# Layer 3's attention: causal masks of the weights by GpSimd selects, and the division's transposes one step later

## The chip, the cores and the metric

The kernel runs on one core of a Trainium2 chip. Its engines are named here as in the profile: PE is TensorE (PEld its weight loads), DVE is VectorE, ACT is ScalarE, POOL is GpSimd, SP is SyncE. Each works through its own queue in order, and they wait for each other through semaphores. The metric is the device time of one execution in microseconds (us), as the median of several runs.

## The reference

The reference is a chain of four layers on x of shape 16 x 256 x 128 (sequences of 256 tokens). Each layer normalises x and adds an attention-like part and a feed-forward part, both computed from the same normalised x. The change concerns the attention of layer 3, which is causal with 16 heads of 8 columns:

```python
q, k, v = (proj(Wq), proj(Wk), proj(Wv))
scores = jnp.einsum('bhsd,bhtd->bhst', q, k)
mask = jnp.triu(jnp.ones((S, S), dtype=bool), k=1)
scores = jnp.where(mask, -jnp.inf, scores)
attn = jax.nn.softmax(scores / sqrt(D), axis=-1)
out = jnp.einsum('bhst,bhtd->bhsd', attn, v)
```

Layer 1 has the same kind of attention, and the kernel uses the same function `attention` for both. The third layer's feed-forward part follows its attention in the program.

## The kernel before

The 16 sequences lie in 8 blocks of two. `attention` goes over 16 half-blocks `(i, bl)`, one sequence each, in a software pipeline: in pass `s` of its loop, `now` is the half-block whose maxima are taken, `last` (the one before) gets its weights, and `old` (two before) gets its context. The 16 half-blocks need 18 passes. The queues of PE, ACT and DVE keep the order in which the code is written (`manual_schedule`).

The keys of a sequence are cut into 4 chunks of 64. The parts are worked in three steps, each with some of the chunks, so that only the lower triangle and the blocks on its diagonal are computed:

- `maxima` (L857) forms the scores with queries on the partitions (tile `sc`), and DVE takes the largest of each row from them (`M`, L878). Step 0 handles chunk 3, step 1 chunks 2 and 0, step 2 chunk 1. After step 2 the maxima are copied, negated, to `negm` (L882).
- `shift` (L887) transposes `negm` by PE (`mT`, L893), and DVE adds it to the queries (`Q2`, L899 and L902). From here on the row's maximum is taken off by the matmul itself.
- `weights` (L904) forms the scores again, now with keys on the partitions (tile `se`), and ACT takes the exponential of them (`E`, L920) from PSUM to SBUF, in two halves `n` of 2 groups of heads. Step 0 handles chunk 0, step 1 chunks 3 and 1, step 2 chunk 2. `E` has one buffer for each step.
- `context` (L922) multiplies the `vals` by `E` of all three steps (tile `av`), in the order step 0, step 1 twice, step 2; a column of ones in `vals` gives the sum of the weights. ACT copies the result to `cu` (L935).
- `divide` (L937) transposes `cu` by four PE transposes (L942), and DVE takes the reciprocal of the sums (L947) and multiplies (L948) into `cx`. `turn` (L953) transposes a block's `cx` once both halves are there (`cxT`, L957).
- `project` (L799) makes the queries, keys and values of the next block, in five portions (`pq` twice, `pk` twice, `pv`), which are put between the steps. A pass with an even `s` has both portions `pq` and the turn, one with an odd `s` both portions `pk` and `pv`. ACT copies them to `Qp` (L810), `Qm` (L812), `Kp` (L817) and `vals` (L833), and DVE makes `Km` from `Kp` (L819). The last two half-blocks have no projections beside them.

Both `maxima` and `weights` call `score` (L836). All PE matmuls go through `mm` (L111). After its matmuls, `score` adds the causal mask to the diagonal blocks by four more matmuls: `pick`, a selector, times `after` or `before`, a 64 x 64 triangle of -1e30, both in bf16. They accumulate into the same PSUM tile and close its accumulation:

```python
for g in (0, 2, 1, 3):
    r = slice(64 * (g // 2), 64 * (g // 2) + 64)
    o = cut(tiles[g // 2][:, g % 2, :])
    ...
    mm(o, pick[r], m.to_broadcast([64, *o.shape[1:]]), False, True)
```

PSUM is divided into two single banks, which `av`, `cu`, `pq`, `pk`, `pv` and `cxT` take in turn, and three pairs of banks, which `sc` (two pairs a step), `se` (two pairs a step) and `mT` (one) take in turn. A tile can be written only when the tile three turns earlier has been read.

In the loop, step 0 of a pass issues the maxima of `now`, the context of `old`, the weights of `last`, the division of `old`, and a portion of the projection; step 1 the maxima, a portion and the weights; step 2 the maxima, a portion or a turn, and the weights; then comes the shift. In layer 3 `beside` adds small reductions on DVE (`gx`, L1133) between the steps of the first passes.

Of the kernel before, what the change touches and what calls it, by code (L numbers as in the profile page):

```python
# [13 lines left out]
ALU = mybir.AluOpType  # L14
# [5 lines left out]
B, S, D = 16, 256, 128  # L20
NBLK = 8
NT = 4
E = 8
# [28 lines left out]
def program(ctx: ExitStack, tc: tile.TileContext, x, consts, consts0, rows, pk0, w0s, w0e, pk1, pk1i, pk2, pk3, out):  # L52
    nc = tc.nc
# [6 lines left out]
    def bank(name):  # L60
        return psum["now"].tile([P, 512], F32, tag="ps", name=name)

    def pair(name):
        return psum["pairs"].tile([P, 2, 512], F32, tag="pr", name=name)
# [45 lines left out]
    def mm(o, l, r, start=True, stop=True):  # L110
        nc.tensor.matmul(o, l, r, start=start, stop=stop)  # L111
# [43 lines left out]
    for n in range(2):  # L155
        t = cp.tile([P, 4, 2, 4, 2, 16], F32, tag=f"negm{n}", name=f"negm{n}")
# [5 lines left out]
    for n in range(2):  # L162
        t = cp.tile([P, 8, 8, 2, 16], F32, tag=f"vals{n}", name=f"vals{n}")
# [5 lines left out]
    pick, after, before = (cp.tile([P, n], BF16, tag=k, name=k) for k, n in (("pick", 128), ("after", 64), ("before", 64)))  # L169
# [19 lines left out]
    with early, banks(8, 0), tc.tile_pool(name="l0", bufs=2) as sp:  # L189
# [15 lines left out]
        for hf in range(2):  # L205
# [3 lines left out]
            n = TILES * SLOTS // P  # L209
# [196 lines left out]
        parts = {}  # L406
# [283 lines left out]
        with tc.manual_schedule(engines=ordered):  # L690
# [10 lines left out]
            for n in range(4):  # L701
                nc.sync.dma_start(
                    out=yT[:, :, 4 * n : 4 * n + 4, :],
                    in_=ycd.rearrange("d (h b t) -> d h b t", h=2, b=B)[:, :, 4 * n : 4 * n + 4, :],
                )
        with tc.manual_schedule(engines=ordered | {mybir.EngineType.Pool}):
# [7 lines left out]
            for k in range(NJ):  # L714
                if k + AHEAD < NJ:
                    fetch_weights(k + AHEAD)
                n = k - TILES - 1
# [66 lines left out]
    def attention(ap_, kp_, blocks, w, layer, beside=iter(())):  # L784
# [51 lines left out]
        def score(tiles, lhs, rhs, parts, wide, cut, mask):  # L836

            for T in range(2):
                for c, at, k0, k1 in parts:
                    for g in range(4):  # L840
                        r = slice(32 * g, 32 * g + 32)
                        o = T * wide + at
                        mm(
                            tiles[g // 2][:, g % 2, o : o + k1 - k0],
                            lhs[r, T, c].rearrange("p j k -> p (j k)"), rhs[r, T, k0:k1], T == 0 and at == 0, False,
                        )
            for g in (0, 2, 1, 3):
                r = slice(64 * (g // 2), 64 * (g // 2) + 64)
                o = cut(tiles[g // 2][:, g % 2, :])
                m = mask[r]  # L850
                for _ in o.shape[1:-1]:
                    m = m.unsqueeze(1)
                mm(o, pick[r], m.to_broadcast([64, *o.shape[1:]]), False, True)
# [33 lines left out]
        def shift(i, bl):  # L887

            t, name, o = blk[i], f"{layer}_{i}_{bl}", bl * S
            ps = pair(f"mT_{name}")  # L890
            for T in range(2):
                for c in range(4):
                    nc.tensor.transpose(  # L893
                        ps[:, T, c * P : (c + 1) * P], negm[bl][:, c, T].rearrange("p g j k -> p (g j k)"), ident
                    )
            Q2 = t["Q2", bl] = ap_.tile([P, 2, S], F32, tag="Q2", name=f"Q2_{name}")
            q2 = Q2.rearrange("p t (c q) -> p t c q", c=4)
            mT = ps.rearrange("p t (c j q) -> p t c j q", c=4, j=2)
            nc.vector.tensor_tensor(  # L899
                q2, t["Qp"][:, :, o : o + S].rearrange("p t (c q) -> p t c q", c=4), mT[:, :, :, 0, :], ALU.add  # L900
            )
            nc.vector.tensor_tensor(q2, q2, mT[:, :, :, 1, :], ALU.add)  # L902

        def weights(i, bl, step):  # L904

            t, name = blk[i], f"{layer}_{i}_{bl}"
            parts, cut = (
                (((0, 0),), lambda a: halves(a)[:, :, 0:64]),
                (((3, 0), (1, 64)), lambda a: halves(a)[:, :, 0:128].rearrange("p t (n c) -> p t n c", n=2)),
                (((2, 0),), lambda a: halves(a[:, 0:256])[:, :, 0:64]),  # L910
            )[step]
            se = [pair(f"se{step}{n}_{name}") for n in range(2)]
            wide = 128 if step == 2 else 256
            E = t["E", bl, step] = ap_.tile([P, 4, 2 * wide], F32, tag=f"E{step}", name=f"E{step}_{name}", bufs=1)
            score(
                se, t["Km"][:, :, 4 * bl : 4 * bl + 4], t["Q2", bl],
                [(c, at, 64 * c, S) for c, at in parts], wide, cut, before,
            )
            for n in range(2):
                nc.scalar.activation(E[:, 2 * n : 2 * n + 2, :], se[n][:, :, 0 : 2 * wide], AF.Exp, scale=ISQ)  # L920

        def context(i, bl):  # L922
            t, name = blk[i], f"{layer}_{i}_{bl}"
            ps = bank(f"av_{name}")
            for n, (c, step, at, wide) in enumerate(((0, 0, 0, 256), (1, 1, 64, 256), (3, 1, 0, 256), (2, 2, 0, 128))):
                nq = 256 - 64 * c
                for T in range(2):
                    for g in range(4):
                        mm(
                            ps[32 * g : 32 * g + 32, (T + 1) * S - nq : (T + 1) * S],  # L930
                            vals[i % 2][:, 4 * bl + c, 4 * T + g].rearrange("p j k -> p (j k)"),
                            t["E", bl, step][:, g, T * wide + at : T * wide + at + nq], n == 0 and T == 0, n == 3 and T == 1,
                        )
            cu = t["cu", bl] = ap_.tile([P, 2, S], F32, tag="cu", name=f"cu_{name}")
            nc.scalar.copy(cu, ps.rearrange("p (t q) -> p t q", t=2))  # L935

        def divide(i, bl):  # L937
            t, name = blk[i], f"{layer}_{i}_{bl}"
            ps = bank(f"cu_{name}")
            for c in range(2):  # L940
                for T in range(2):
                    nc.tensor.transpose(  # L942
                        ps[:, (2 * c + T) * P : (2 * c + T + 1) * P], t["cu", bl][:, T, c * P : (c + 1) * P], ident
                    )
            p3 = ps.rearrange("p (h k) -> p h k", k=16)
            rd = ap_.tile([P, 32, 1], F32, tag="rd", name=f"rd_{name}")
            nc.vector.reciprocal(rd, p3[:, :, 8:9])  # L947
            nc.vector.tensor_tensor(  # L948
                t["cx"][:, 2 * bl : 2 * bl + 2, :].rearrange("p c (h k) -> p (c h) k", k=8), p3[:, :, 0:8],
                rd.to_broadcast([P, 32, 8]), ALU.mult,  # L950
            )

        def turn(i):  # L953
            name = f"{layer}_{i}"
            ps = transpose4(blk[i]["cx"], f"cxT_{name}")
            cT[i] = kp_.tile([P, 512], F32, tag="cT", name=f"cT_{name}", bufs=NBLK)
            nc.scalar.copy(cT[i], ps)  # L957

        seqs = [(i, bl) for i in blocks for bl in range(2)]
        with tc.manual_schedule(engines={mybir.EngineType.PE, mybir.EngineType.Activation, mybir.EngineType.DVE}):  # L960
            for _ in project(blocks[0]):
                pass
            coming = iter(())
            turns = []
            for s in range(len(seqs) + 2):
                now, last, old = (seqs[k] if 0 <= k < len(seqs) else None for k in (s, s - 1, s - 2))
                if now and now[1] == 0 and now[0] != blocks[-1]:
                    coming = project(blocks[blocks.index(now[0]) + 1])
                for step in range(3):
                    if now:  # L970
                        maxima(*now, step)
                    if step == 0 and old:
                        context(*old)
                    if step == 2 and s % 2 == 0:
                        if turns:
                            turn(turns.pop())
                    elif step > 0:
                        next(coming, None)
                    if last:
                        weights(*last, step)  # L980
                    if step == 0:
                        if old:
                            divide(*old)
                            if old[1] == 1:
                                turns.append(old[0])
                        next(coming, None)
                    if step < 2:
                        next(beside, None)
                if now:
                    shift(*now)  # L990
                next(beside, None)
            for i in turns:
                turn(i)
# [119 lines left out]
    with tc.tile_pool(name="l3w", bufs=1) as wp:  # L1113
# [31 lines left out]
        with banks(4, 0), tc.tile_pool(name="l3t", bufs=4, space=PSUM, reuse_waits="tile") as tp, \  # L1145
                tc.tile_pool(name="l3", bufs=2, reuse_waits="tile") as sp:
            base = wp.tile([P, B], F32, tag="base", name="base")
# [345 lines left out]
```

## Time and profile before

| what | value |
|---|---|
| median of 3 runs | 1593.74 us (1591.17 to 1594.62) |
| the profiled execution's own time | 1487.93 us |
| its span, first to last instruction | 1486.2 us |
| granted TensorE clock over the span | 0.94 of full speed |
| layer 3's attention in the span | about 1085 to 1386 us |
| one pass with `pq` at full clock (1300.77 to 1316.97) | 16.2 us |
| one pass with `pk` at full clock (1182.46 to 1199.56) | 17.1 us |

The profile is that of one execution. It gives the busy time of each engine, the waits of one engine for another, the chain of work that ended last, and a timeline of all instructions. In a timeline row stand the start in us from the span's start, the duration in us (with idle time inside a merged row left out or not much), the engine, the line, the operation, the tiles written and read with their shapes, the count, and in brackets the idle time of the engine just before it and what ended that. PEld rows are the better guide to PE's order, since the ends of matmuls are modelled. The profiled execution is shorter than the runs that give the median.

### The profile page before, as it was taken

What the parts mean: (1) busy time and instruction counts of PE and PEld (TensorE: products, weight loads), DVE (VectorE), ACT (ScalarE), POOL (GpSimd) and SP (SyncE); (2) the same over time, 40 slices, a digit from 0 to 9 for tenths busy, and PEclk for the clock granted to TensorE, in tenths of its full rate; (3) what the DMA queues carried; (4) which work ended last, traced back from release to release, by engine and by line L of the source; (5) the groups of instructions that cost most, each with busy time, mean ns of one, the idle gap of its engine ahead of it and who ended that gap; (6) DMA issues with size and microseconds to landing.
All of it is one profiled execution on the core that took longest, in us unless ns stands there. A gap on an engine that the chain in (4) does not pass through costs nothing.

```text
span 1486.2 us, 28149 instructions
## 1 busy us (share of the span) xinstructions
PE 1340.1 (90%) x11950; PEld 868.6 (58%) x11950; DVE 752.8 (51%) x1636; ACT 578.4 (39%) x898; POOL 214.3 (14%) x218
## 2 busy tenths in 40 slices
PE   3659999969898999899999999999979999999995
PEld 3546899836565666656555445554546666666434
DVE  7355444756666555335732336423375565554364
ACT  5412223334353554321343334333344545543551
POOL 1366004323110000000220112211100000000013
PEclk9979999977798999899999999999978999997998
DMA  7849669640000000000000000000000000000001
GB/s 225 283 135 312 205 178 278 197 152 21 10 11 2 2 2 2 2 1 1 0 1 0 1 0 1 0 0 0 0 1 2 2 2 2 2 2 2 1 1 57
DMA packets 71007, 77.92 MB, mean 52 GB/s; under 512 B 7649, under 2 KB 60258, under 8 KB 70242
## 3 DMA queue, kind: packets, MB, share of 16 engines
q1 hardware_dynamic: 66210, 66.39, 14.5%
q0 software_dynamic: 4240, 8.99, 1.8%
q8 instruction: 94, 1.54, 0.4%
q10 hardware_dynamic: 432, 0.75, 0.2%
q14 instruction: 31, 0.25, 0.1%
HBM read 55.46 MB, written 20.64 MB: 51 GB/s over the span
## 4 chain that ended last, share of the span: by engine, by line
PE 79%; DVE 10%; ACT 7%; issue 2%; DMA 1%; POOL 1%; POOLq 0%; DVEq 0%; SPq 0%; ACTq 0%
PE h L111 15%; PE se L111 9%; PE sc L111 8%; PE po L111 7%; PE av L111 5%; ACT E L920 4%; DVE M L878 3%; PE c L111 3%; PE mT L893 3%; PE sy L111 3%; PE sg L111 2%; PE su L111 2%; PE pq L111 2%; PE pv L111 2%; PE b L111 2%; PE a L111 2%
## 5 line engine op out<-in xcount | busy, mean ns | idle before, releaser
L878 DVE TENSOR_REDUCE M<-sc 128x4 f32<-128x1024 f32 (+3 forms) x256 | 195.9, 818 | 105.0 <-PE sc L111 105.0
L111 PE MATMUL h<-h,pk 128*128 128x512 f32 x512 | 221.0, 592 | 0.0
L920 ACT ACTIVATE E<-se 128x1024 f32<-128x1024 f32 (+1 forms) x192 | 158.8, 879 | 126.0 <-PE se L111 125.7
L111 PEld LDWEIGHTS h<-h,pk 128*128 128x128 f32 x512 | 97.3, 190 | 119.0 <-issue 114.8
L111 PE MATMUL sc<-Kp,Qm 32*128 32x192 f32 (+3 forms) x2048 | 139.8, 358 | 25.0 <-ACT E L920 19.9
L111 PE MATMUL se<-Q,Km 32*128 32x256 f32 (+3 forms) x2048 | 138.4, 355 | 22.4 <-DVE M L878 20.9
L111 PEld LDWEIGHTS sc<-Kp,Qm 32*128 32x128 f32 x2048 | 103.5, 207 | 74.6 <-ACT E L920 33.4
L111 PEld LDWEIGHTS se<-Q,Km 32*128 32x128 f32 x2048 | 99.3, 202 | 62.9 <-issue 51.8
L1098 ACT ACTIVATE h<-h,pk 128x512 f32<-128x512 f32 x64 | 44.0, 687 | 144.3 <-PE h L111 144.2
L1048 POOL TENSOR_TENSOR pr<-q,k 128x512 f32<-128x512 f32 (+2 forms) x24 | 28.3, 1205 | 495.7 <-ACT k L1041 285.8
L601 POOL DMA_INDIRECT yk<-YS,slots x64 | 60.7, 949 | 225.9 <-DMA YS<-ys 95.0
L1108 DVE TENSOR_TENSOR x<-x,po 128x512 f32<-128x512 f32 x8 | 5.5, 688 | 170.5 <-PE po L111 170.5
L111 PE MATMUL av<-E,vals 128*32 128x256 f32 (+3 forms) x2048 | 77.7, 304 | 0.0
L389 POOL DMA_INDIRECT XS<-xn,slots x64 | 63.0, 985 | 73.4 <-DVE slots L368 48.3
L1240 POOL TENSOR_TENSOR xT<-xT,c 128x512 f32<-128x512 f32 x8 | 10.2, 1271 | 389.8 <-DVE c L1239 380.4
L935 ACT COPY cu<-av 128x512 f32<-128x512 f32 x32 | 18.8, 586 | 120.6 <-PE av L111 120.6
L111 PEld LDWEIGHTS av<-E,vals 128*32 128x32 f32 x2048 | 52.9, 111 | 20.0 <-issue 1.6
L583 DVE TENSOR_TENSOR hs<-hs,su 128x512 f32<-128x512 f32 x46 | 31.6, 686 | 57.3 <-PE su L111 57.3
L899 DVE TENSOR_TENSOR Q<-Qp,mT 128x512 f32<-128x512 f32 x32 | 22.0, 688 | 58.0 <-PE mT L893 58.0
L111 PE MATMUL pk<-xT,pk 128*128 128x512 f32 x80 | 47.0, 672 | 3.8 <-ACT Qm L812 3.7
L819 DVE TENSOR_SCALAR Km<-Kp,consts 128x512 f32<-128x512 f32 x64 | 32.2, 545 | 34.6 <-ACT Kp L817 34.6
L111 PEld LDWEIGHTS sy<-we,hs 128*128 128x128 f32 x368 | 47.6, 192 | 2.4 <-DVE hs L583 0.5
(276 smaller groups left out, 2259.0 us busy)
## 6 DMA issues: line engine op xcount, KB each, us to landing
we<-in_w0e SPq DMA_DIRECT2D x46, 384.0 KB, 3.9
toe<-kd SPq DMA_DIRECT2D x32, 512.0 KB, 6.8
xs<-XS SPq DMA_DIRECT2D x46, 128.0 KB, 4.4
YS<-ys SPq DMA_DIRECT2D x46, 128.0 KB, 2.6
XS<-Z SPq DMA_DIRECT2D x4, 1024.0 KB, 9.8
pk<-in_pk SPq DMA_DIRECT2D x1, 3145.5 KB
x<-in_x SPq DMA_DIRECT2D x8, 256.0 KB, 5.2
ycd<-yc SPq DMA_DIRECT2D x8, 256.0 KB, 8.4
```

The lines of the kernel that those rows point to most:

```text
L111: nc.tensor.matmul(o, l, r, start=start, stop=stop)
L389: d = nc.gpsimd.indirect_dma_start(out=XS[hf][:, :], out_offset=at_rows(slots[:, hf, k, n : n + 1]), in_=xn[HALVES[hf][n // NT]][:, n % NT ...
L583: nc.vector.tensor_tensor(h, h, pu, ALU.mult)
L601: nc.gpsimd.indirect_dma_start(out=y, out_offset=None, in_=YS[hf][:, :], in_offset=at_rows(slots[:, hf, k, n : n + 1]),)
L819: nc.vector.tensor_scalar(t["Km"][:, T, :, j, :], chunks(t["Kp"][:, T, :]), C["hmask"][:, j : j + 1], C["hone"][:, j : j + 1], ALU.mult, A ...
L878: nc.vector.tensor_reduce(dst, src, AX.X, ALU.max, negate=True)
L893: nc.tensor.transpose(ps[:, T, c * P : (c + 1) * P], negm[bl][:, c, T].rearrange("p g j k -> p (g j k)"), ident)
L899: nc.vector.tensor_tensor(q2, t["Qp"][:, :, o : o + S].rearrange("p t (c q) -> p t c q", c=4), mT[:, :, :, 0, :], ALU.add)
L920: nc.scalar.activation(E[:, 2 * n : 2 * n + 2, :], se[n][:, :, 0 : 2 * wide], AF.Exp, scale=ISQ)
L935: nc.scalar.copy(cu, ps.rearrange("p (t q) -> p t q", t=2))
L1048: nc.gpsimd.tensor_tensor(pr[:, :, j:], q[:, :, j:], k[:, :, 0 : S - j], ALU.mult)
L1098: nc.scalar.activation(hn[:, c, :], ps, AF.Gelu, scale=W2[sn][:, c : c + 1])
```

## The change

In layer 3 alone (`late`), `score` is called without a mask for the weights, and the last ordinary matmul closes the accumulation. The exponential is thus taken of unmasked scores. After each of its two halves, POOL sets the entries above the diagonal to zero in place, with `affine_select` on each diagonal block: one instruction for each half of the partitions (`j`), over 2 groups, 2 tiles of heads and 64 queries. That makes 4 of them in step 0, 8 in step 1 and 4 in step 2. The maxima keep their masks, and so does all of layer 1.

Also in layer 3, `divide` is called at the end of step 1, after the weights of step 1, instead of in step 0 after the weights of step 0. So its transposes stand on PE between `se` of step 1 and `sc` of step 2, and its two DVE instructions between the maxima of step 1 (and `Km`) and those of step 2. The single banks are taken in the new order.

```diff
@@ score @@
-                            lhs[r, T, c].rearrange("p j k -> p (j k)"), rhs[r, T, k0:k1], T == 0 and at == 0, False,
+                            lhs[r, T, c].rearrange("p j k -> p (j k)"), rhs[r, T, k0:k1], T == 0 and at == 0,
+                            mask is None and T == 1 and at == parts[-1][1],
                         )
+            if mask is None:
+                return
             for g in (0, 2, 1, 3):
@@ attention @@
+        late = layer == 3
@@ weights @@
-                [(c, at, 64 * c, S) for c, at in parts], wide, cut, before,
+                [(c, at, 64 * c, S) for c, at in parts], wide, cut, None if late else before,
             )
             for n in range(2):
                 nc.scalar.activation(E[:, 2 * n : 2 * n + 2, :], se[n][:, :, 0 : 2 * wide], AF.Exp, scale=ISQ)
+                if late:
+                    for _, at in parts:
+                        d = E.rearrange("p g (t q) -> p g t q", t=2)[:, 2 * n : 2 * n + 2, :, at : at + 64]
+                        for j in range(2):
+                            r = slice(64 * j, 64 * j + 64)
+                            nc.gpsimd.affine_select(
+                                out=d[r], in_=d[r], pattern=[[0, 2], [0, 2], [1, 64]], compare_op=ALU.is_ge, fill=0.0,
+                                base=0, channel_multiplier=-1,
+                            )
@@ the loop @@
                     if last:
                         weights(*last, step)
+                    if old and step == (1 if late else 0):
+                        divide(*old)
+                        if old[1] == 1:
+                            turns.append(old[0])
                     if step == 0:
-                        if old:
-                            divide(*old)
-                            if old[1] == 1:
-                                turns.append(old[0])
                         next(coming, None)
```

## The prediction

> **What bounds the kernel now.** I read the page first (engine shares, clock), then the waits and the timeline of layer 3's attention (1085 to 1386 us of the span).
>
> ```profile
> PE 1340.1 (90%) x11950; PEld 868.6 (58%) x11950; DVE 752.8 (51%) x1636; ACT 578.4 (39%) x898; POOL 214.3 (14%) x218
> PE 79%; DVE 10%; ACT 7%; issue 2%; DMA 1%; POOL 1%; POOLq 0%; DVEq 0%; SPq 0%; ACTq 0%
> ```
>
> PE is the engine to shorten; POOL runs nothing between the last product of layer 2 and 1408.7 us, so the whole attention of layer 3 has an idle GpSimd. A busy PE is not yet a bound, so I ask what PE waits for in this stage (columns: us in total, times, longest):
>
> ```profile
> PE sc L111 <- ACT E L920: 9.7, 13, 0.8
> PE se L111 <- DVE M L878: 4.2, 9, 1.1
> PE mT L893 <- DVE negm L882: 3.2, 5, 2.5
> ```
>
> Three short waits recur: the third maxima (sc of step 2) wait for the exponentials of step 1, because the three pairs of banks go round; the second weights wait for the maxima; the transposes mT wait for negm. One period at full clock, from av at 1300.77 to the next av at 1316.97, shows where they lie:
>
> ```profile
> 1303.22 0.59 ACT L935 COPY cu<-av 128x512 f32<-128x512 f32 x1 [3.78 <-PE av L111]
> 1304.16 0.11 PEld L111 LDWEIGHTS <-pick 64*128 64x128 bf16 x4 [0.33 <-issue]
> 1304.38 0.42 PEld L942 LDWEIGHTS cu<-consts,cu 128*128 128x128 f32 x4
> 1304.54 1.94 ACT L920 ACTIVATE E<-se 128x1024 f32<-128x1024 f32 x2 [0.73 <-PE se L111]
> 1304.77 0.30 PEld L111 LDWEIGHTS pq<-xT,pk 128*128 128x128 f32 x2
> ...
> 1310.24 0.11 PEld L111 LDWEIGHTS <-pick 64*128 64x128 bf16 x4 [0.22 <-issue]
> 1310.57 0.30 PEld L111 LDWEIGHTS sc<-Kp,Qm 32*128 32x128 f32 x4 [0.21 <-issue]
> 1310.73 1.94 ACT L920 ACTIVATE E<-se 128x1024 f32<-128x1024 f32 x2 [0.41 <-PE se L111]
> 1311.81 0.52 PEld L111 LDWEIGHTS sc<-Kp,Qm 32*128 32x128 f32 x12 [0.94 <-ACT E L920]
> ...
> 1314.10 0.39 DVE L882 COPY negm<-M 64x32 f32<-64x32 f32 x2
> 1314.16 0.11 PEld L111 LDWEIGHTS <-pick 64*128 64x128 bf16 x4
> 1314.61 0.86 PEld L893 LDWEIGHTS mT<-consts,negm 128*128 128x128 f32 x8 [0.33 <-PE se L111]
> ```
>
> The four masks of a step hold PE for 0.22 us (1304.16 to 1304.38) or 0.33 us (1310.24 to 1310.57), and delay the exponential behind them; the division's transposes hold PE for 0.39 us (1304.38 to 1304.77) where PE has other work ready; and a hole of about 0.8 us lies just before 1311.81, where it has none.
>
> **What the Trainium skill says.** "Perfetto Trace Analysis", section "GPSIMD Engine Instruction", asks that POOL be timed by start-to-start spacing and not by the reported span. I do so below; here both agree within 0.1 us. "GPSIMD Engine Reference", section 2.1, says that a core of GpSimd goes on to the next instruction once its own 16 partitions are done, so the selects on partitions 0 to 63 and 64 to 127 might overlap. The trace does not support it: the four 64-partition memsets of L166 start 0.24 to 0.28 us apart and last 0.20 to 0.24. I count no overlap. Section 8 there says that GpSimd contends with VectorE instructions that have two SBUF inputs or a two-port mode. The trace agrees: L1069 takes 1.73 us beside POOL and 0.68 without. In this stage DVE's maxima and divisions read PSUM, and Km (L819) reads one tensor at about one element per cycle (541 ns for 512), so I take no slowdown.
>
> **The change part by part.** In layer 3 it removes 12 masks per half-block (4 in each of 3 steps, 16 half-blocks, 192 in all), adds 4, 8 and 4 selects per half-block (256 in all) on POOL, and moves four transposes, one reciprocal and one product from step 0 to the end of step 1. No DMA moves and SP's queue is untouched. In the built order context's first matmuls of each E wait for POOL, and so does the next exponential into the same E, which context precedes anyway.
>
> *Period with pq (the one shown).* Step 0: 0.22 of masks and 0.39 of transposes leave, so pq and sc of step 1 come 0.61 earlier. The maxima follow, and se of step 1 ends at 1310.24 - 0.61 = 1309.63. The exponential then starts about 0.13 us later (as the copy of av starts 0.13 after the next load, 1303.09 to 1303.22) instead of 0.49 later: 1309.76; ACT is free of Qm at 1310.32 - 0.61 = 1309.71. Its first half lets sc go on 1.08 later, at 1310.84 instead of 1311.81: 0.97 gained. The transposes (0.39) fit into the hole and cost nothing; were the hole gone they would cost their 0.39. Step 2: its mask of 0.22 gives nothing, because the maxima of step 2 and negm (until 1314.49) end last; they move with sc. Gain 0.95.
>
> *Period with pk* (av at 1182.46 to 1199.56). PE again gains 0.6 in step 0, but the chain exponential E0 (1186.23) - Kp - Km - first maxima (until 1190.89) - se sets the time, and only the mask ahead of E0 shortens it: 0.25. PE's wait for M grows instead. At step 1 the mask's 0.36 is added. Gain 0.6. DVE has room for the division there: it idles 1.87 us before the maxima of step 2 at 1194.85, and reciprocal and product take 0.36 + 0.42.
>
> *Sum of PE's side.* 7 periods with pk x 0.6, 6 with pq x 0.95, and the two without projections x 0.6 (they wait for E and M as the pk periods do): 4.2 + 5.7 + 1.2 = 11.1 us.
>
> *The selects.* The trace has no select; its nearest rows, in the timeline of POOL:
>
> ```profile
> 1463.79 0.41 POOL L1268 TENSOR_TENSOR m<-xn,b 128x128 f32<-128x128 f32 x1 [12.03 <-DVE b L1218]
> 1464.16 0.77 POOL L1268 TENSOR_TENSOR m<-xn,nb 128x128 f32<-128x128 f32 x2
> 1465.37 1.05 POOL L1269 TENSOR_TENSOR xn<-xn,a 128x512 f32<-128x512 f32 x1
> 1466.38 0.41 POOL L1268 TENSOR_TENSOR m<-xn,b 128x128 f32<-128x128 f32 x1
> ```
>
> Each select covers 64 partitions x 256 elements. From below: memsets of 1024 start 0.89 apart, 0.87 ns an element, with 0.16 fixed: 0.38 us. From the middle: products L1268 of 128 start 0.37 apart and L1269 of 512 1.01, so 0.16 + 1.67 ns an element: 0.58 for 256 with two inputs. "GPSIMD Engine Reference", section 7, gives 1.03 to 2.03 cycles per element for compare-and-select code, an estimate of 0.38 to 0.59 with 1.2 GHz and 0.16 fixed. From above: the nb form of L1268 takes 0.85 for only 128. I take d = 0.5, with 0.38 and 0.85 as ends.
>
> *What hides them.* In the pq period the first half of E1 is ready at about 1310.8; then 8 selects of E1 and 4 of E2 follow on POOL. Context starts at 1316.97 - 0.95 = 1316.0 and comes to E2 after about 1.8 us of its 2.3: 1317.8. So 12d must fit in 7.0: d up to 0.58. In the pk period 1193.2 to 1200.7 gives 0.62. At d = 0.5 the cover holds. If it is gone, each period loses 12 x (d - 0.6), and everything behind context on PE (se of step 0, then ACT and DVE) is late by it. The gain is used up at about d = 0.6 + 0.75 / 12 = 0.66.
>
> *The end.* The last half-block has no maxima beside it: the first half of E1 is ready at about 1379.3, context wants E2 at about 1382, and 12d = 6.0 ends at 1385.3. Against the end of av before (1383.2) this puts the end about 2.6 later (1.4 at 0.4, 3.7 at 0.59).
>
> Sum: -11.1 + 2.6 = -8.5 us on a profiled execution of 1487.93 us (span 1486.2). The median of the runs, 1593.74, is 1.071 times that; no view shows why, but where the clock is low in this trace (0.74 to 0.90 in some periods) masks take 0.40 instead of 0.28, so the saving should stretch about as much: -9. **Forecast 1585.**
>
> **The rivals.** *POOL is late* (slower). One mechanism: d above 0.66, so that context waits for the last selects of E2 in each period. At d = 0.75: 12 x 0.15 = 1.8 less 0.75 is +1.05 a period, x 15 = 16, plus about 5.5 at the end: +21, 1615. At 0.85: +34 and 6.5, 1634. For it: POOL's slow 0.85 us product, and that runs of 64 in a four-dimensional pattern may cost more than a memset's. Against it: a select has one input, and the two-input row gives 0.58. *Nothing left* (within noise): d near 0.63 to 0.66, or Km doubled by POOL's port traffic in the seven pk periods; in full, at the 2.5 times of L1069, it would cost 7 x 1.5 = 10 and undo the gain: about 1593. *The change doesn't do what it says*: excluded by the built order, in which the 192 masks are gone and the transposes stand after se of step 1 (in layer 1 nothing moves).
>
> **How the numbers follow.** The noise of a measurement of this kernel is about 0.2%, 3 us. Gain with cover: 0.58, its own range 1579 to 1590 (d from 0.4 to 0.6, low clock in more periods). Nothing left: 0.09. POOL late: 0.33, of which about half lies below 1616. Range 1576 to 1616: leaves out some 0.17 above and 0.02 below. The likeliest is the gain, 1585.
>
> **What would show it.** Right: selects starting under 0.6 us apart; no wait of av for POOL beyond the last half-block; the wait of sc for E down from 9.7 to a few us while that of se for M grows; periods of about 15.3 (pq) and 16.5 us (pk) at full clock instead of 16.2 and 17.1; negm still the last before mT. Wrong: a wait "av <- POOL E" of a microsecond or more in every period (POOL late), Km well over 541 ns (contention), or sc of step 2 waiting as long as before although the transposes stand there.

## The result

The changed kernel takes 1581.54 us (median of 11 runs, 1579.75 to 1586.72) against 1593.28 us before on the same chip (11 runs). The ratio is 0.9939 with a 95% interval of 0.9914 to 0.9964, which is 9.7 us less, between 5.7 and 13.7. Here and below a saving in us is this ratio applied to the median before; the medians themselves differ by some us more or less than that (here by 11.7 us). The forecast was 1585, 8.7 us less than its base of 1593.74.

The profiled execution of the changed kernel took 1582.27 us (span 1580.6). It is not to be set beside the 1486.2 us of the span before: the products `s` of layer 2 start at 830.1 us here and at 723.8 us before, so the difference had arisen ahead of layer 2, where the change touches nothing. From there to the last of them it is 321.5 us in both. It goes with the chip: the kernel before takes 1593.23 us (median) on the chip of e1 to e4, but 1487.86 and 1489.71 us on those of e5 to e8 and of e9 and e10. What follows compares layer 3's attention alone, pass by pass.

The page of the changed kernel, engine shares and the row of the selects:

```profile
PE 1353.3 (86%) x11758; PEld 872.0 (55%) x11758; DVE 755.0 (48%) x1636; ACT 577.1 (37%) x898; POOL 318.9 (20%) x474
L932 POOL TENSOR_SCALAR_AFFINE_SELECT E<-E 64x256 f32<-64x256 f32 x256 | 105.8, 413 | 211.4 <-ACT E L925 200.1
```

There are 192 matmuls less on PE and 256 more instructions on POOL, at 413 ns each. The idle time of POOL ahead of them is nearly all waiting for ACT. What PE waits for in the attention of layer 3 (total, times, longest), first before (1085 to 1386 us), then in the changed kernel (1178 to 1478 us):

```profile
PE sc L111 <- ACT E L920: 10.8, 15, 0.8
PE se L111 <- DVE M L878: 5.3, 10, 1.1
PE mT L893 <- DVE negm L882: 3.2, 5, 2.5
```

```profile
PE se L111 <- DVE M L881: 8.6, 10, 1.1
PE mT L896 <- DVE negm L885: 7.6, 14, 2.5
PE sc L111 <- ACT E L925: 2.4, 3, 0.9
PE av L111 <- POOL E L932: 2.0, 3, 1.3
```

(The prediction shows 9.7 and 4.2 us for the first two before: its rows are those of a window from 1085 to 1345 us, and not to 1386.) The wait of `sc` for the exponentials has gone from 10.8 to 2.4 us. The waits for the maxima and for `negm` have grown in its place, and `av` waits for POOL only three times, all in the last half-block. One pass with `pq`, and the one with `pk` behind it, in the timeline:

```profile
1277.47 1.94 ACT L925 ACTIVATE E<-se 128x1024 f32<-128x1024 f32 x2
1277.48 0.42 PEld L957 LDWEIGHTS cu<-consts,cu 128*128 128x128 f32 x4 [0.23 <-issue]
1278.06 0.30 PEld L111 LDWEIGHTS sc<-Kp,Qm 32*128 32x128 f32 x4 [0.17 <-issue]
1278.54 0.52 PEld L111 LDWEIGHTS sc<-Kp,Qm 32*128 32x128 f32 x12 [0.18 <-ACT E L925]
1278.56 5.54 POOL L932 TENSOR_SCALAR_AFFINE_SELECT E<-E 64x256 f32<-64x256 f32 x12 [3.65 <-ACT E L925]
...
1280.84 0.52 DVE L885 COPY negm<-M 64x32 f32<-64x32 f32 x2
1281.47 0.86 PEld L896 LDWEIGHTS mT<-consts,negm 128*128 128x128 f32 x8 [0.69 <-PE se L111]
...
1283.78 2.11 PEld L111 LDWEIGHTS av<-E,vals 128*32 128x32 f32 x64
...
1289.81 1.19 DVE L819 TENSOR_SCALAR Km<-Kp,consts 128x512 f32<-128x512 f32 x2 [3.53 <-ACT Kp L817]
1290.92 2.47 DVE L881 TENSOR_REDUCE M<-sc 128x4 f32<-128x768 f32 x4
...
1292.31 1.10 PEld L111 LDWEIGHTS se<-Q,Km 32*128 32x128 f32 x28 [0.96 <-issue]
```

The transposes `cu` now lie where the hole was: the load of `sc` waits 0.18 us for E instead of 0.94. The twelve selects from the first half of E1 on take 5.54 us, 0.46 each, and end at 1284.1, 1.5 us before context comes to E2. In the pass with `pk` the loads of `se` stand idle for 0.96 us (PE's matmuls for 0.85) until the maxima behind Km are done, as foreseen.

The passes from one start of `av` to the next were read from the timelines of all profiles. The 16 starts bound 15 passes. The first twelve have projections beside them, six with `pq` and six with `pk`; the table has these twelve. "Full clock" is the length to which most agree within 0.03 us; the last column is what the twelve have above it in all.

| kernel | pq, full clock | pk, full clock | passes over 0.2 us longer | surplus |
|---|---|---|---|---|
| before | 16.19 | 17.10 | 4 | 6.1 us |
| e5_before_again | 16.19 | 17.10 | 5 | 7.6 us |
| changed | 15.35 | 16.59 | 1 | 1.5 us |
| e1_masks_only | 15.55 | 16.59 | 4 | 6.5 us |
| e2_move_only | 15.97 | 17.10 | 0 | 0.0 us |
| e4_no_selects | 15.19 | 16.36 | 0 | 0.0 us |
| e6_step2_and_last_on_PE | 15.35 | 16.59 | 0 | 0.0 us |
| e7_Km_later, e8_both | 15.36 | 15.79 | 0 | 0.0 us |
| e9_filler | 16.19 | 17.10 | 0 | 0.0 us |

So the twelve passes lost 12.6 us between the two profiles: 6 x 0.84 and 6 x 0.51, which is 8.1 us, at full clock, and 4.6 us of surplus. The second part was not in the forecast. The last three passes took 2.3 us less, at a clock of 0.74 to 0.99 in both profiles, and the end behind them took 3.2 us more. In all, from the first start of `av` to the first loads of the next stage, 255.2 us became 243.5. The experiments are about these parts. (Where the expectations of e5 and e6 count 15 passes up to a "sixteenth start of av", their figures are those of 14 passes and of the fifteenth start.)

### The profile page after: what moved, and what is told of

Same layout as the page of the kernel before. It is cut to its first block, busy times and chain, and to the rows that moved or that the text cites. A ratio compares the mean times of both kernels' runs of the same rounds, so it can differ in the third digit from the quotient of the medians.

```text
span 1580.6 us, 28021 instructions
## 1 busy us (share of the span) xinstructions
PE 1353.3 (86%) x11758; PEld 872.0 (55%) x11758; DVE 755.0 (48%) x1636; ACT 577.1 (37%) x898; POOL 318.9 (20%) x474
## 4 chain that ended last, share of the span: by engine, by line
PE 74%; DVE 10%; ACT 6%; issue 5%; another core or an unknown queue 4%; POOL 1%; DMA 1%; POOLq 0%; DVEq 0%; SPq 0%; ACTq 0%
PE h L111 14%; PE sc L111 7%; PE se L111 7%; PE po L111 7%; PE av L111 5%; DVE M L881 4%; PE c L111 3%; ACT E L925 3%; PE mT L896 3%; PE sg L111 3%; PE sy L111 2%; PE su L111 2%; PE pq L111 2%; PE a L111 2%
## 5 line engine op out<-in xcount | busy, mean ns | idle before, releaser
L111 PE MATMUL sc<-Kp,Qm 32*128 32x192 f32 (+3 forms) x2048 | 138.7, 357 | 26.3 <-ACT E L925 20.9
L932 POOL TENSOR_SCALAR_AFFINE_SELECT E<-E 64x256 f32<-64x256 f32 x256 | 105.8, 413 | 211.4 <-ACT E L925 200.1
L111 PE MATMUL cv<-toe,Z 128*32 128x128 f32 x512 | 34.3, 347 | 29.9 <-issue 29.7
L111 PE MATMUL sg<-xsT,we 128*128 128x256 f32 x184 | 49.4, 392 | 5.4 <-ACT xsT L572 5.4
L896 PE MATMUL mT<-consts,negm 128*128 128x128 f32 x256 | 40.7, 310 | 14.4 <-DVE negm L885 8.5
```

What stands on the lines that cost most here:

```text
L896: nc.tensor.transpose(ps[:, T, c * P : (c + 1) * P], negm[bl][:, c, T].rearrange("p g j k -> p (g j k)"), ident)
L932: nc.gpsimd.affine_select(out=d[r], in_=d[r], pattern=[[0, 2], [0, 2], [1, 64]], compare_op=ALU.is_ge, fill=0.0, base=0, channel_multiplie ...
```

## The experiments

The theory from the prediction is that the masks and the transposes leave PE's path in two separate places, that POOL's selects are covered by 7.0 to 7.5 us of other work in each pass, and that they show only at the end.

**One part at a time.** e1_masks_only puts the division back into step 0:

```diff
-                    if old and step == (1 if late else 0):
+                    if old and step == 0:
```

> The changed kernel with the division back in step 0, so only the masks are exchanged for selects. Theory (two separate gains, each read from one pass): a pass with pq loses 0.22 of masks in step 0 and about 0.36 in step 1, and pays back about 0.1 because DVE's copies to negm are slower beside POOL: 15.7 us instead of 16.2; a pass with pk is set by E0 - Kp - Km - M and loses 0.25 + 0.36 less 0.1: 16.6 instead of 17.1, as in the changed kernel. The hole of about 0.75 us before the third maxima stays. In all about -7 us in the passes and +2.5 at the end: some 5 us below the kernel before. Rival (the division's move brings nearly all of it): passes of 16.1 and 17.0, and no gain or a loss in all.

Measured: ratio 0.9954 (0.9936 to 0.9972), 7.3 us less than before; passes of 15.55 and 16.59 us. The theory's 15.7 and 16.6 are near, and the rival's 16.1 and 17.0 are excluded. In the timeline of one of its passes the hole is still there:

```profile
1312.83 0.33 PEld L111 LDWEIGHTS sc<-Kp,Qm 32*128 32x128 f32 x4
1312.95 1.94 ACT L925 ACTIVATE E<-se 128x1024 f32<-128x1024 f32 x2
1314.02 0.52 PEld L111 LDWEIGHTS sc<-Kp,Qm 32*128 32x128 f32 x12 [0.87 <-ACT E L925]
```

e2_move_only keeps the masks on PE, leaves out the selects, and moves the division:

```diff
-                [(c, at, 64 * c, S) for c, at in parts], wide, cut, None if late else before,
+                [(c, at, 64 * c, S) for c, at in parts], wide, cut, before,
-                if late:
+                if False:
                     for _, at in parts:
```

> The kernel before with only the division moved to the end of step 1 in layer 3; masks stay on PE and there are no selects. Theory: the transposes' 0.39 us leaves step 0 and lies in the hole of step 1, so a pass with pq takes 15.8 us instead of 16.2; a pass with pk stays at 17.1, because E0, which starts the chain that sets it, is not earlier. In all about -2.5 us, hardly to be told from no change by the times, but clear in the passes. Rival: passes of 15.4 and 16.6, as in the changed kernel.

Measured: ratio 0.9958 (0.9935 to 0.9982), 6.7 us less; passes of 15.97 and 17.10 us. For `pk` the theory holds; for `pq` only 0.22 of the 0.39 us came. The transposes do fit into the hole whole: the loads of `sc` behind them still wait 0.35 us for the exponential. The rest is lost at the scores of step 1, which PE now reaches 0.40 us earlier. They need a pair of banks that step 0's exponential, which comes no earlier, is still reading (its first half ends 1297.78 in one such pass): half of their first matmuls start only at 1297.83, 0.18 us behind the others, and their 32 loads take 1.36 us instead of 1.19. At full clock the two parts add: 0.64 + 0.22 is the changed kernel's 0.84 within 0.02 for `pq`, 0.51 + 0 its 0.51 for `pk`. But six passes at 0.22 make 1.3 us, and the times show 6.7, with 2.9 as the least that the interval allows. The surplus of the twelve passes, 6.1 us before and none here, is of the size of the rest. That led to e5_before_again and e9_filler.

**The price of the selects.** e3_selects_twice issues each select twice:

```diff
                         for j in range(2):
                             r = slice(64 * j, 64 * j + 64)
-                            nc.gpsimd.affine_select(
+                            for _ in range(2):
+                                nc.gpsimd.affine_select(
```

> The changed kernel with each select issued twice (the second changes nothing), so that POOL has 24 instead of 12 selects between the first half of E1 and the last of E2. Theory (selects 0.46 us apart one after the other, covered for 7.0 to 7.5 us in each pass): 24 x 0.46 = 11.0 us need 3.5 to 4 us more than the cover, so passes of about 19.3 (pq) and 20.1 us (pk), with av waiting for POOL in each; 15 passes and 5.5 us at the end make it about 60 us slower than the changed kernel, about 50 slower than the kernel before. Rival (the two halves of the partitions overlap on different cores of GpSimd, so that a pair costs hardly more than one): under 20 us slower than the changed kernel.

Measured: ratio 1.0406 (1.0352 to 1.0460), 65 us slower than before; passes of 19.4 to 20.9 (`pq`) and 22.5 to 22.7 us (`pk`). The rival of overlapping selects is excluded, and with twice the selects the prediction's own rival, that POOL is late, comes true: `av` waits for POOL 52.2 us in 47 waits. Every second pass with `pq` ran at full clock, in 19.43 us, which is the theory's 19.3; the other passes cost more than the theory's 3.5 to 4 us. Windows around one of the waits (1289.90 to 1292.70), with PE's busy time, granted clock, DMA share and GB/s, show what they have beside the wait:

```profile
1286.10:1288.40 2.30, 1.35 (x32) 1.00 0.01 4
1289.90:1292.70 2.80, 1.29 (x16) 0.64 0.00 0
1292.70:1295.00 2.30, 2.30 (x19) 0.50 0.03 7
```

After PE has waited here, the work behind the wait runs at half the clock: `se` of step 0 takes 2.09 us instead of 1.15. Whether low clock is all that the passes with `pk` have above 20.1 us wasn't taken apart.

e4_no_selects leaves the selects out, so that weights above the diagonal stay in; only its time counts:

```diff
-                if late:
+                if False:
                     for _, at in parts:
```

> The changed kernel without any select: the weights of layer 3 above the diagonal stay in. Only the price of the selects is meant. Theory: they cost the wait at the end (about 2.3 us) and about 0.1 us a pass through slower DVE copies: 4 us faster than the changed kernel, passes of 15.25 and 16.5 us, negm copies together back to 0.39 us. Rival (selects hold the passes in some other way, through semaphores or the order on ACT): 8 us or more faster than the changed kernel, passes under 15.0 and 16.2.

Measured: ratio 0.9881 (0.9842 to 0.9920) against 0.9939, some 9 us less than the changed kernel, but the two intervals overlap, so the times can't tell the theory's 4 us from the rival's 8; passes of 15.19 and 16.36 us. So all selects of a pass cost 0.16 (`pq`) and 0.23 us (`pk`) although context never waits for them in these passes, about twice what was expected, and the rival's passes under 15.0 and 16.2 are excluded. Where it goes is seen on DVE: the two copies to `negm`, on whose end `mT` waits, take 0.39 us in all again (0.52 beside POOL), and the first pair of Km 1.00 (1.19 beside POOL).

**The clock.** e5_before_again is the kernel before once more, for a second profile.

> The kernel before once more, for a second profile of its passes. Over its 15 passes (first to sixteenth start of av) the granted clock was 0.93 and the time 241.8 us; the kernel with the masks exchanged but the hole before the third maxima left had 0.93 as well, while the three kernels with the transposes in that hole had 0.96. Theory (PE's idle 0.8 us in each pass brings clock dips with it): 0.92 to 0.94 again, 239 to 243 us, with 4 or 5 passes more than 1 us over their full-clock length. Rival (the clock of one execution is chance): it may as well be 0.96, with one or two such passes.

Measured (one execution, 1492.68 us; this chip's median for the kernel before is 1487.86 us): a clock of 0.93 over 242.4 us, as the theory has it, and five of the twelve passes longer than at full clock, four of them by more than 1 us, by 7.6 us in all. Of the three profiles with the hole, 13 of 36 passes are too long; of the profiles of the changed kernel, e2 and e4, which have it filled, 1 of 36. The records of the granted clock show why only some passes are hit. In these three profiles every stretch at half clock in layer 3's attention lasts 3.41, 6.83 or 10.24 us, and within one execution all begin on one grid with steps of 3.41 us. Three such steps of the kernel before; the columns are busy time of PE, PEld, DVE, ACT and POOL, then clock, DMA share and GB/s:

```profile
1136.88:1140.29 3.41, 3.36 (x42) 1.85 (x43) 3.06 (x5) 2.73 (x5) 0.00 (x0) 1.00 0.00 0
1140.29:1143.70 3.41, 2.35 (x38) 1.69 (x36) 1.22 (x3) 1.94 (x2) 0.00 (x0) 1.00 0.02 5
1143.70:1147.11 3.41, 3.41 (x28) 2.59 (x26) 1.20 (x5) 1.08 (x2) 0.00 (x0) 0.50 0.00 0
```

In the second of them PE idles 1.06 us, the hole of 0.75 and another of 0.31, and the third runs at half clock. Twelve stretches begin in the 36 passes; in the step before each PE idles 0.75 to 1.33 us in all (its ends are modelled), and in the steps that no low clock follows 0.96 at most. In e2 and e4, with the hole filled, no step of the twelve passes has more than 0.67. So what seems to count is how much of the holes falls into one step, and the hole alone lies on the border. The idle time is not the whole rule: in e3, steps with up to 1.53 us of it were followed by full clock. No run moved the holes against the grid.

That profiles with the hole have low clock might still come from the other edits. e9_filler tests this: it takes nothing away from the kernel before, and adds useless work.

```diff
             wide = 128 if step == 2 else 256
+            if step == 2 and layer == 3:
+                for c in range(4):
+                    nc.tensor.transpose(sc[0][:, 0, c * P : (c + 1) * P], t["Qp"][:, 0, c * P : (c + 1) * P], ident)
             score(
```

> The kernel before with four useless transposes of 128 x 128 on PE in layer 3 just ahead of the third maxima, written into their bank and overwritten by them: the division stays in step 0 and all masks stay. Work is added and none is taken away. Theory (it is PE's idle hole there that brings the low clock with it): the passes keep their full-clock length, 16.2 and 17.1 us, since the transposes' 0.6 us fits into the hole of 0.75 to 0.94; but nearly none of the 12 passes with projections is longer than that, where the kernel before had 4 and 5 such passes worth 6.1 and 8.7 us. So the kernel is 5 to 8 us faster than before. Rival (the low clock has another cause, such as the masks or the number of matmuls): as many long passes as before, and the same time or 1 us more.

(The 8.7 us in it is a slip; the twelve passes of e5_before_again add to 7.6.) Measured: ratio 0.9950 (0.9932 to 0.9969), 7.4 us faster than before with 64 transposes more. The passes are 16.19 and 17.10 us as before, and not one of the twelve is longer. A part of one of its passes, and a window over its twelve passes and 0.8 us behind them (clock 1.00; in the kernel before 0.96 over the 205.84 us of its twelve):

```profile
1189.51 0.42 PEld L871 LDWEIGHTS sc<-consts,Qp 128*128 128x128 f32 x4 [0.21 <-issue]
1189.67 1.94 ACT L923 ACTIVATE E<-se 128x1024 f32<-128x1024 f32 x2 [1.97 <-PE se L111]
...
1190.75 0.52 PEld L111 LDWEIGHTS sc<-Kp,Qm 32*128 32x128 f32 x12 [0.35 <-ACT E L923]
```

```profile
1129.85:1330.37 200.52, 194.20 (x3064) 131.93 (x3064) 116.58 (x197) 103.27 (x149) 0.00 (x0) 1.00 0.01 2
```

The rival is excluded: nothing but the work in the hole has changed. So PE's hole (0.75 us between matmuls, 0.94 between loads) cost nothing but itself in most passes, and about one pass in three with it was longer through low clock, by 0.2 to 2.3 us. "TensorE: Matmul & The Clock Gate" in the Trainium skill, section "HAM oscillation — how this bites in real kernels", gives as an abstract rule that PE should have no idle gaps of more than about 3.4 us. Here much shorter holes did it, so the measurement decides: in these traces 3.4 us is the step of the clock's records, not the length of the hole.

**What ends the passes now.** e6_step2_and_last_on_PE returns to PE the masks of step 2 and all those of the last half-block:

```diff
-                [(c, at, 64 * c, S) for c, at in parts], wide, cut, None if late else before,
+                [(c, at, 64 * c, S) for c, at in parts], wide, cut, None if late and step < 2 and (i, bl) != seqs[-1] else before,
-                if late:
+                if late and step < 2 and (i, bl) != seqs[-1]:
```

> The changed kernel with the masks back on PE in step 2 of all half-blocks, and in all steps of the last half-block; POOL selects steps 0 and 1 of the first 15. Theory (step 2's masks on PE cost nothing, since mT waits for negm anyway, and the wait at the end goes): passes as in the changed kernel, 15.35 and 16.6 us, and from the sixteenth start of av to the next stage's first matmuls 13.9 instead of 16.4 us (of which 0.7 was low clock there): some 2 to 3 us faster than the changed kernel. Rival (each mask on PE costs its 0.22 us wherever it stands): passes 15.55 and 16.8, 3 us lost in the passes, nothing gained in all.

Measured: ratio 0.9871 (0.9845 to 0.9898) against the kernel before on its own chip; passes of 15.35 and 16.59 us. The masks of step 2 on PE are free, to 0.01 us, because `mT` waits for `negm` longer than they last. The wait at the end is gone: from the sixteenth start of `av` to the first loads of the next stage it is 4.82 us, as in the kernel before, where the changed kernel takes 8.02. Whether in all it beats the changed kernel by the 2 to 3 us expected can't be told: its interval lies below the changed kernel's (0.9914 to 0.9964), by more than was expected, but the two were measured on different chips.

e7_Km_later moves the four Km on DVE:

```diff
-                for j in range(2):
-                    nc.vector.tensor_scalar(t["Km"][:, T, :, j, :], ...)
+                if not late:
+                    ones_in(t, T)
+                elif T == 1:
+                    ones_in(t, 0)
                 yield
...
+            if late:
+                ones_in(t, 1)
             yield
```

> The changed kernel with DVE's two pairs of Km in layer 3 issued later: the first pair after the maxima of step 1 instead of ahead of them, the second after the maxima of step 2 and the copies to negm. Km is wanted only two passes later. Theory (in passes with pk the chain E0 - Kp - Km - M - se sets the time): se no longer waits 0.85 us for M, and a pass with pk takes 15.75 us instead of 16.6; passes with pq stay at 15.35; about 6 us faster than the changed kernel. Rival (DVE has no room behind step 1: the division and the maxima of step 2 come later by as much, or something else ends the pass): pk passes of 16.3 us or more, less than 2 us gained.

Measured: ratio 0.9889 (0.9862 to 0.9917); passes with `pk` of 15.79 us instead of 16.59, those with `pq` unchanged. In the timeline the maxima come straight behind `sc`, Km behind them, and `se` no longer waits:

```profile
1212.97 2.49 DVE L889 TENSOR_REDUCE M<-sc 128x4 f32<-128x768 f32 x4 [3.83 <-PE sc L111]
1214.37 1.10 PEld L111 LDWEIGHTS se<-Q,Km 32*128 32x128 f32 x28 [0.16 <-issue]
1215.37 0.99 DVE L801 TENSOR_SCALAR Km<-Kp,consts 128x512 f32<-128x512 f32 x2
```

The chain E0, Kp, Km, M, `se` of the prediction is thus confirmed: an order on DVE, not PE's work, set the pass with `pk`. The 6 us expected against the changed kernel can't be checked by the times, for the same reason as with e6.

e8_both joins the edits of e6 and e7.

> The edits of e6_step2_and_last_on_PE and e7_Km_later together. Theory: they lie in different waits, so the gains add: passes of 15.35 (pq) and 15.75 us (pk), and the shorter end; some 8.5 us faster than the changed kernel, about 18 us faster than the kernel before. Rival (Km behind the copies to negm stands in the way of Q2, or the mask of step 2 is no longer free once the pass is shorter): no more than the better of the two alone.

Measured: ratio 0.9863 (0.9826 to 0.9900); passes of 15.35 and 15.79 us, and 4.82 us at the end (8.02 in e7), so at full clock the gains add. The times can't confirm it: the interval takes in that of e6 and overlaps that of e7, and e8 isn't shown to be faster than either.

e10_both_layers adds, in layer 1, the division's move and the later Km (`late` is dropped from the conditions of both). Layer 1's masks stay on PE.

> e8_both with the division's move and the later Km in layer 1 too (its masks stay on PE, since POOL fetches there). In layer 1 of the kernel before the passes were 16.2 and 17.1 us at full clock, with 7 of the first 12 longer than that by 0.7 to 7.3 us. Theory: there too the hole is filled and Km leaves the chain, so pq passes of 15.97 and pk passes of 16.6 us at full clock and few of the long ones, 5 to 12 us faster than e8_both. Rival (in layer 1 DVE has the combines and norms of the layer before between the steps, so its order decides and the moves give nothing or harm): within 3 us of e8_both, or slower.

Measured: ratio 0.9707 (0.9669 to 0.9745), 1443.31 us against 1489.71: faster than the kernel before by 43.6 us by the ratio, and the only version here whose interval lies below those of all others. Layer 1's passes at full clock are 15.97 and 16.49 us (16.19 and 17.10 before), and the first twelve together take 203.2 us instead of 225.6. Against e8_both (on another chip) that is 1.6% or some 23 us, twice the most that was expected: 6 x 0.22 and 6 x 0.61 make 5 us of the 22 in these passes, and the rest lies in long passes that have become shorter. The granted clock over these twelve passes is 0.99 instead of 0.91: 3.4 us at half clock instead of 41.0, which can be worth up to 19 us. So the clock can account for the rest, but how much is clock and how much DVE's order among the combines of layer 0 wasn't taken apart.

## Why the prediction was right, and where it was not

- **Direction and size:** right; 8.7 us forecast, 9.7 measured. That they lie so near is in part luck: one gain was missing from the sum (the clock), the gains of both passes were too good by 0.1 us, and the end costs more than forecast. The profiles give -8.1 for the twelve passes at full clock (the forecast's terms give -9.3 for them), -4.6 of clock there, -2.3 in the last three passes (the forecast's other terms give -1.8), and +3.2 at the end.
- **The passes:** 15.3 and 16.5 us were forecast at full clock, 15.35 and 16.59 came. Gains of 0.95 and 0.6 were forecast; 0.84 and 0.51 came, and 1.00 and 0.74 without the selects (e4), so what is lacking is the selects' doing. e1 and e2 show the gains of masks and move separately, with the hole in step 1 and the chain of Km where the timeline had put them.
- **Nothing from step 2's masks:** right, and shown by e6.
- **The selects:** d = 0.5 was taken; the spacing is 0.46 us, inside the 0.38 to 0.59 that was estimated from the cycles in the Trainium skill ("GPSIMD Engine Reference", section 7). (The upper end of 0.85 was read from L1268's `nb` form; the row shown has two of these in 0.77 us, and it is the other three pairs, at 1.67 us each, that give 0.85.) No overlap of the partition halves: right, shown by e3. Cover of 7.0 us and more: it held in every pass but the end. e3, with 11 us of selects, shows what lay behind it.
- **"I take no slowdown" on DVE:** the step that failed on the side of the cost. Copies to `negm` and Km became slower beside POOL (0.39 to 0.52 us, 1.00 to 1.19); one Km in four took 0.74 us instead of 0.54, which the prediction had named as a sign of being wrong. By e4 that is 0.16 to 0.23 us a pass, some 3 us in 15 passes. The prediction ruled it out because Km reads one tensor at about one element per cycle. The trace before does not bear that out: maxima of 256, 512 and 768 elements start 0.33, 0.61 and 0.87 us apart, 1.05 ns for each further element, but a Km of 512 starts only 0.46 us before the next. So Km is faster than that rate, and the two-port mode that the prediction names was not ruled out for it. That this mode is the cause is not shown: no run varies it.
- **The end:** +2.6 forecast. From the sixteenth start of `av` to the next stage's first loads it is 8.02 us instead of 4.82, both at full clock, so +3.2; without selects in the last half-block (e4, e6) it is 4.82 again. Two of the waits of PE there:

```profile
1473.53 1.35 PE L111 MATMUL av<-E,vals 128*32 128x192 f32 x32 [1.34 <-POOL E L932]
1475.41 0.63 PE L111 MATMUL av<-E,vals 128*32 128x128 f32 x12 [0.53 <-POOL E L932]
```

- **The stretch by 1.071:** wrong. It was laid to a low clock in layer 3; the extra time lies ahead of layer 2, goes with the chip, and has nothing to do with the change. It added only half a microsecond.
- **The missing term:** the hole was priced as 0.8 us of idle time that the transposes could use. In about one pass in three it also brought low clock to what followed. That is 4.6 us between the two profiles, and, by e9, about 7 us by the times without any other change.

## What to carry to other kernels

Read what each stage waits for, and put work that must be done anyway into PE's short waits: here it paid twice, once where the work was and once through the clock. When masks or other small steps go to an idle engine, count how many of them lie between their input and their first reader, at start-to-start spacing, and compare that with the other work in between; the price shows where the pipeline runs out, at its end. And look at the order on the engine that PE waits for: an instruction wanted only two passes later (Km) held the pass by 0.8 us.

## What the runs showed of the hardware that was not expected

- Idle holes of TensorE of about 0.75 us in each pass went with stretches at half the granted clock: 13 of 36 passes with such a hole were longer, 1 of 36 without in the profiles of the changed kernel, e2 and e4, none of 12 with useless transposes in it. The stretches last 3.41 us or two or three times that, on one grid in an execution, and in these passes each follows a step of 3.41 us in which PE idled 0.75 us or more.
- Around a wait of 1.5 us for POOL (e3) the clock was 0.64 on the mean, and 0.50 behind it.
- A select of 64 partitions x 256 elements takes 0.41 us on GpSimd, 0.46 from start to start, and two on different halves of the partitions do not overlap.
- DVE's copies from SBUF to SBUF (`negm`, two of 64 x 32 elements: 0.39 to 0.52 us; Km, two of 128 x 512 with a product: 1.00 to 1.19) become slower beside GpSimd's selects. Its products `cx` and the adds with `mT`, which read PSUM, do not: 0.42 and 0.69 us with and without.
